# The gate's nonlinearity beside attention: a Silu lookup in place of tanh and a multiply

## The chip, the core and the metric

The kernel runs on one core of a Trainium2 chip. A core has five engines with queues of their own: TensorE (PE, matmuls; its weight loads are listed as PEld), VectorE (DVE), ScalarE (ACT), GpSimd (POOL) and SyncE (SP, which issues transfers). [...] Matmuls write to PSUM, a memory of banks[...]; the rest of the work is in SBUF. The metric is the device time of one execution in microseconds. A row of the profile names the line of the kernel and the tiles that it writes and reads (`hl<-sl,hh`).

## What is computed

The input has 4096 tokens of 256 features. The reference chains three residual blocks: half an FFN, attention, half an FFN again with the same weights.

```python
x = x + 0.5 * ffn(layernorm(x), ...)
x = x + attn(layernorm(x), ...)
x = x + 0.5 * ffn(layernorm(x), ...)

# in ffn
gate = jax.nn.silu(jnp.einsum('ech,ehi->eci', xg, rg))     # routed: 8 experts, top 2, capacity 640
up = jnp.einsum('ech,ehi->eci', xg, ru)
eout = jnp.einsum('eci,eih->ech', gate * up, rd)
...
shared = jax.nn.silu(x @ sg) * (x @ su) @ sd               # shared: 256 -> 2048 -> 256
return shared + SCALE * routed.reshape(b, s, h)

# in attn: groups of 64 tokens, 16 heads of 16
att = jnp.einsum('bghqd,bghkd->bghqk', q, k) * scale
att = jnp.where(causal, att, -jnp.finfo(att.dtype).max)
att = jax.nn.softmax(att, axis=-1)
y = jnp.einsum('bghqk,bghkd->bghqd', att, v)
```

silu(g) is g * sigmoid(g), which is also g/2 * (1 + tanh(g/2)).

## The kernel before

Tokens are worked on in blocks of 512 (`BT`) and tiles of 128. Every operand of a matmul is held as two fp16 planes, high and low, and a product is three matmuls (`TERMS`: high by high, high by low, low by high).

The program has four stages. Stage a: layernorm and routing of the first FFN (tiles `tile1`) with the shared FFN of blocks 0 to 3 beside them. Stage b: the eight experts of the first FFN. Stage c: attention (32 tiles, `tile2`, which also do layernorm and routing of the second FFN), with eleven blocks of shared FFN beside it: blocks 4 to 7 of the first FFN and 0 to 6 of the second. Stage d: the experts of the second FFN and the shared FFN of its last block. The change concerns stage c alone.

A block of the shared FFN is 16 chunks of 128 hidden features (`shared`). For a chunk, `gate_up` issues six matmuls for the gate into one PSUM tile `pgu`, then the nonlinearity into `sl`, then six matmuls for the up half into another `pgu`; line 319 multiplies the two on VectorE, line 321 casts to fp16 (`hh`, ScalarE), line 322 makes the low plane (`hl`, VectorE). The twelve down matmuls of a chunk (`down`, line 330) are issued one chunk late (`defer`), so that they follow the next chunk's gate and up. There are three PSUM tiles for `pgu`, two of `sl` and two pairs of `hh` and `hl`. A gate's PSUM tile is free for other matmuls when the last reader of the gate is done.

`gate_up` has two forms of the nonlinearity. With `tanh=True`, the form of stage c, ScalarE looks up tanh(g/2) (line 313), and VectorE computes (tanh + 1) * g from it (line 314); the factor 1/2 is folded into line 319. Otherwise ScalarE looks up Silu itself (line 317).

`attn_tile` is a generator: each `yield` ends a step of one attention tile. Its softmax subtracts the row maximum on GpSimd (line 550), takes the exponential on ScalarE (line 558, 128x1024), casts it to fp16 (line 560, ScalarE), makes the low plane on GpSimd (line 561) and transposes both by DMA (line 564). Other work of a tile on ScalarE: squares with a sum (line 498), casts of q and k (521, 527), copies of v (554, four of 64x512), layernorm's scaling (154) and casts (164, 505). `Tiles` starts a new tile every four slots, and `drive` takes two side steps for each step of the shared FFN and begins a slot every three.

Within the source order so given, the order on each engine is laid out by a scheduler when the kernel is built (`schedule_with_timeline_sim=True`, line 825); it also puts single matmuls of attention between those of a chunk.

ScalarE looks functions up in tables. The compiler puts an instruction that loads a table (ACT_TABLE_LOAD) ahead of a lookup where the loaded table lacks its function; the source has no such line, and the profile gives it the line of that lookup.

Of the kernel before, what the change touches and what calls it, by code (L numbers as in the profile page):

```python
# [14 lines left out]
AF = mybir.ActivationFunctionType  # L15
ALU = mybir.AluOpType
# [10 lines left out]
XP = UP * WS  # L27
# [10 lines left out]
class Net:  # L38
# [254 lines left out]
            R["sc"] = True  # L293
            self.tc.add_to_no_dep_group(R["key"], i)

    def gate_up(self, wc, x, h, tanh=False):

        nc = self.nc
        n = x.shape[-1]
        ps = []  # L300
        for i in range(2):
            p = self.ps_gu.tile([P, n], F32, name="pgu", tag="gu")
            j = 0
            for k in range(2):
                for (w, a) in TERMS:
                    nc.tensor.matmul(  # L306
                        p, lhsT=wc[:, w, i, k, :], rhs=x[:, 2 * a + k, :], start=(j == 0), stop=(j == 5))
                    j += 1
            ps.append(p)
            if i == 0:  # L310
                s = self.hp.tile([P, BT], F32, name="sl", bufs=self.nsl)[:, :n]
                if tanh:
                    nc.scalar.activation(s, p, AF.Tanh, scale=0.5 / XP)  # L313
                    nc.vector.scalar_tensor_tensor(  # L314
                        out=s, in0=s, scalar=1.0, in1=p, op0=ALU.add, op1=ALU.mult)
                else:
                    nc.scalar.activation(s, p, AF.Silu, scale=1.0 / XP)  # L317
                yield
        nc.vector.scalar_tensor_tensor(  # L319
            out=s, in0=ps[1], scalar=1.0 / XP / (2.0 * XP if tanh else 1.0), in1=s, op0=ALU.mult, op1=ALU.mult)  # L320
        nc.scalar.copy(h[0], s)  # L321
        nc.vector.tensor_tensor(out=h[1], in0=s, in1=h[0], op=ALU.subtract)  # L322
        yield
# [22 lines left out]
            res.append(r)  # L346
        return res

    def shared(self, b, xb, src, dst, tanh=False, late=2):
        nc = self.nc  # L350
        outs = [self.ps_out.tile([P, BT], F32, name="po", tag="po") for _ in range(2)]
        for c in range(16):
            if c == late:
                res = self.res_load(src, b)
            h = [a[:, 0:BT] for a in self.hbuf()]
            yield from self.gate_up(self.sgu[:, c], xb, h, tanh)

            def fin(c=c, h=h):
                self.down(outs, 4, h, self.sdw[:, :, c], c, 16)
                if c < 15:  # L360
                    return
                for i in range(2):
                    nc.vector.scalar_tensor_tensor(
                        out=res[i], in0=outs[i].rearrange("p (t f) -> p t f", f=H), scalar=0.5 / WS,
                        in1=res[i], op0=ALU.mult, op1=ALU.add)
                    nc.sync.dma_start(
                        out=dst[b * BT + i * 2 * P:b * BT + (i + 1) * 2 * P].rearrange("(t p) f -> p t f", p=P),
                        in_=res[i])

            self.defer(fin)  # L370
            yield
# [299 lines left out]
def run_slots(tiles, until):  # L671
    while not until():
        for _ in tiles.steps():
            pass


def drive(main, tiles, rate):

    credit = 0.0
    side = iter(())  # L680
    for _ in main:
        credit += 1.0
        for _ in range(2):
            if next(side, "end") == "end":
                break
        if credit >= rate:
            for _ in side:
                pass
            credit -= rate
            if not tiles.done():  # L690
                side = tiles.steps()
    for _ in side:
        pass


@with_exitstack
def macaron(ctx, tc, x, w_qkv, ln_w, w_proj, router_w, rg, ru, rd, sg, su, sd, out):
    nc = tc.nc
    x = x.rearrange("b s h -> (b s) h")
    out = out.rearrange("b s h -> (b s) h")  # L700
    n = Net(ctx, tc)
    R1 = n.route_init(0)
    R2 = n.route_init(1)
    R2["acc"] = out
    x2 = n.dr.tile([T, H], F32, name="x2")
    fbs = {}
    used = set()

    def new_fb(h, b):
        def get(t):  # L710
            if t == 0:
                assert h == 1 or (1, b) in used
                fb = fbs[(h, b)] = n.front_new()
                fb["pe"] = h == 1 and b < PEB
            return fbs[(h, b)]
        return get

    def tail(R, h, b, t):
        if t == 3:
            yield from n.route(R, b, fbs[(h, b)])  # L720

    def tile1(j):
        b, t = divmod(j, 4)
        y = n.load_tile(x, b, t)
        yield
        yield
        yield from n.front_steps(y, t, new_fb(1, b))
        yield from tail(R1, 1, b, t)

    def tile2(j):  # L730
        b, t = divmod(j, 4)
        yield from n.attn_tile(R1, j, x2 if b < NC else out, new_fb(2, b))
        yield from tail(R2, 2, b, t)

    def ready(h, b):
        return lambda: (h, b) in fbs and fbs[(h, b)]["n"] == 4

    def all_shared(key, b, src, dst, **k):
        yield from n.shared(b, fbs[key]["xb"], src, dst, **k)
        used.add(key)  # L740

    def fill(R):

        for e in range(E):
            z = n.raw.tile([P, 5, XW], F32, name="zero")
            nc.gpsimd.memset(z, 0.0)
            nc.vector.tensor_scalar_add(z[:, :, H], n.tokid[:, 0:5], float(T + e * CAP))
            nc.sync.dma_start(out=R["xg"][e * CAP:(e + 1) * CAP].rearrange("(t p) f -> p t f", p=P), in_=z)
            yield

    with n.phase("a", BT, 2, 10):
        n.ident = n.at.tile([P, P], F32, name="ident")
        make_identity(nc, n.ident)
        n.load_router(router_w)
        tiles = Tiles(tile1, 32, GAP_A)
        run_slots(tiles, ready(1, 0))
        n.load_shared(sg, su, sd)
        for _ in fill(R1):
            pass
        for b in range(NA):  # L760
            run_slots(tiles, ready(1, b))
            if b == 2:
                tiles.extra.append(fill(R2))
                for i in range(NA, NB):
                    nc.sync.dma_start(out=R1["acc"][i * BT:(i + 1) * BT], in_=x[i * BT:(i + 1) * BT])
            drive(all_shared((1, b), b, x, R1["acc"]), tiles, RATE_A)
        run_slots(tiles, tiles.done)
        cur = {}
        for _ in n.expert_load(R1, 0, cur):
            pass  # L770
    with n.phase("b", CAP, 3):
        n.experts(R1, rg, ru, rd, cur)
    with n.phase("c", BT, 2, 6, SLC):
        n.attn_init(w_qkv, ln_w, w_proj)
        tiles = Tiles(tile2, 32, GAP_C)
        for b in range(NA, NB):
            drive(all_shared((1, b), b, R1["acc"], R1["acc"], tanh=True), tiles, RATE_C)
        for b in range(NC):
            run_slots(tiles, ready(2, b))
            drive(all_shared((2, b), b, x2, R2["acc"], tanh=True), tiles, RATE_C)  # L780
        run_slots(tiles, tiles.done)
        cur = {}
        for _ in n.expert_load(R2, 0, cur):
            pass
    with n.phase("d", CAP, 3):
        n.experts(R2, rg, ru, rd, cur)
        for b in range(NC, NB):
            for _ in all_shared((2, b), b, out, out, late=10):
                pass
# [6 lines left out]
RATE_C = 3.0  # L796
# [33 lines left out]
```

## Time and profile before

| | us |
|---|---|
| median of 3 runs | 1857.15 (1856.97 to 1858.42) |
| the profiled execution | 1854.02 |
| its span, first to last instruction | 1852.2 |
| TensorE matmul busy | 1785.9 (96%) |
| VectorE busy | 1259.6 (68%) |
| ScalarE busy | 940.6 (51%) |
| GpSimd busy | 726.0 (39%) |

A profile is of one execution. "Busy" is the time in which an engine ran an instruction; matmuls are pipelined and their ends are modelled, so a busy TensorE is not one at its peak. The granted TensorE clock was 0.998 of full speed. Rows of the costliest groups name line, engine, operation, tiles, shapes and count; then busy us in total and mean ns of one; then the engine's idle time just ahead of them and what ended most of it. The groups of the gate's path in stage c and beside it:

```profile
L306 PE MATMUL pgu<-xb,sgu 128*128 128x512 f16 x3072 | 740.2, 381 | 19.5 <-DVE sl L314 8.5
L321 ACT CAST hh<-sl 128x512 f16<-128x512 f32 (+2 forms) x512 | 272.8, 533 | 540.8 <-DVE sl L319 535.5
L319 DVE SCALAR_TENSOR_TENSOR sl<-pgu,sl 128x512 f32<-128x512 f32 (+2 forms) x512 | 300.6, 587 | 203.4 <-PE pgu L306 183.2
L322 DVE TENSOR_TENSOR hl<-sl,hh 128x512 f16<-128x512 f32 (+2 forms) x512 | 328.4, 642 | 146.4 <-ACT hh L321 145.4
L317 ACT ACTIVATE sl<-pgu 128x384 f32<-128x384 f32 (+1 forms) x336 | 158.8, 473 | 53.8 <-PE pgu L306 30.4
L313 ACT ACTIVATE sl<-pgu 128x512 f32<-128x512 f32 x176 | 103.9, 591 | 36.5 <-PE pgu L306 35.1
```

Lines 306, 319, 321 and 322 hold the work of all stages; lines 313 and 314 that of stage c alone (176 = 11 blocks of 16 chunks).

### The profile page before, as it was taken

Reading aid. Unit: us, or ns where it says so; the run is one execution under the profiler, and the core shown is the slowest. Engines: PE = TensorE matmul, PEld = TensorE weight load, DVE = VectorE, ACT = ScalarE, POOL = GpSimd, SP = SyncE. Lnnn points to the kernel's source line nnn. Section 1 sums busy time; section 2 is a strip of 40 time slices with the busy share of each in tenths; the row PEclk is TensorE's granted clock in tenths of the full one; section 3 lists DMA queues with packets and bytes.
Section 4 is the critical chain, followed back from the end, with each engine's and each line's share of the span. In section 5 each row is a group of like instructions: output and inputs, shape, how many; then the busy total and the mean of one; then the engine's idle time right before and its main releaser. Section 6 shows DMA issues by size and latency. Waiting matters only on the chain.

```text
span 1852.2 us, 37412 instructions
## 1 busy us (share of the span) xinstructions
PE 1785.9 (96%) x13546; PEld 1189.7 (64%) x13546; DVE 1259.6 (68%) x3190; ACT 940.6 (51%) x1991; POOL 726.0 (39%) x943
## 2 busy tenths in 40 slices
PE   6899999999999899999999999999999999999999
PEld 3456557777777556665555656565665677777765
DVE  8666545566666567888888888788765566666643
ACT  4333334555555466666566666666433455555542
POOL 5664430123111334557667575757520011112210
PEclk9999999999999999999999999999999999999999
DMA  9763032555543345657576666756213044445420
GB/s 272 220 161 93 12 78 61 114 121 116 119 107 86 82 81 101 135 104 146 103 140 122 130 130 115 147 104 122 53 34 83 27 106 111 110 109 125 106 47 12
DMA packets 447513, 196.59 MB, mean 106 GB/s; under 512 B 302369, under 2 KB 444381, under 8 KB 447264
## 3 DMA queue, kind: packets, MB, share of 16 engines
q1 hardware_dynamic: 429664, 173.03, 41.6%
q0 software_dynamic: 17664, 21.17, 6.7%
q8 instruction: 106, 1.74, 0.4%
q14 instruction: 79, 0.65, 0.1%
HBM read 81.04 MB, written 52.85 MB: 72 GB/s over the span
## 4 chain that ended last, share of the span: by engine, by line
PE 59%; DVE 11%; POOL 9%; DMA 8%; issue 6%; ACT 4%; SPq 1%; DVEq 0%; POOLq 0%; ACTq 0%
PE pgu L306 38%; PE po L330 19%; POOL xg L287 3%; DVE hl L322 2%; DVE sl L319 2%; DMA xg<-X,di 2%; DVE sl L314 2%; DMA xg<-zero 1%; DMA y<-in_L_attn_x_dram 1%; DMA rs<-in_L_ffn_su_dram 1%; POOL X L285 1%; ACT hh L321 1%; DMA QT<-QK 1%; DVE st L139 1%; ACT V L554 1%
## 5 line engine op out<-in xcount | busy, mean ns | idle before, releaser
L306 PE MATMUL pgu<-xb,sgu 128*128 128x512 f16 x3072 | 740.2, 381 | 19.5 <-DVE sl L314 8.5
L321 ACT CAST hh<-sl 128x512 f16<-128x512 f32 (+2 forms) x512 | 272.8, 533 | 540.8 <-DVE sl L319 535.5
L306 PE MATMUL pgu<-xe,wc 128*128 128x384 f16 (+1 forms) x3072 | 497.1, 299 | 0.6
L306 PEld LDWEIGHTS <-sgu 128*128 128x128 f16 x3072 | 294.1, 98 | 298.1 <-issue 33.0
L319 DVE SCALAR_TENSOR_TENSOR sl<-pgu,sl 128x512 f32<-128x512 f32 (+2 forms) x512 | 300.6, 587 | 203.4 <-PE pgu L306 183.2
L322 DVE TENSOR_TENSOR hl<-sl,hh 128x512 f16<-128x512 f32 (+2 forms) x512 | 328.4, 642 | 146.4 <-ACT hh L321 145.4
L330 PEld LDWEIGHTS <-hh 128*128 128x128 f16 x3328 | 319.6, 98 | 114.8 <-ACT hh L321 18.4
L330 PE MATMUL po<-sdw,hh 128*128 128x256 f16 x2048 | 350.6, 273 | 10.8 <-ACT hh L321 10.0
L306 PEld LDWEIGHTS <-wc 128*128 128x128 f16 x3072 | 300.1, 98 | 94.6 <-issue 2.2
L330 PE MATMUL po<-sdw,hl 128*128 128x256 f16 x1024 | 250.9, 274 | 11.4 <-DVE hl L322 10.6
L330 PE MATMUL po<-wd,hh 128*128 128x256 f16 x1280 | 223.7, 273 | 0.0
L330 PEld LDWEIGHTS <-hl 128*128 128x128 f16 x1664 | 162.6, 98 | 62.3 <-DVE hl L322 28.5
L426 POOL DMA_INDIRECT out_dram<-eo,eid x40 | 64.6, 1616 | 315.2 <-DVE hl L322 247.1
L317 ACT ACTIVATE sl<-pgu 128x384 f32<-128x384 f32 (+1 forms) x336 | 158.8, 473 | 53.8 <-PE pgu L306 30.4
L287 POOL DMA_INDIRECT xg<-X,di x128 | 137.3, 1072 | 89.4 <-DVE di L266 29.9
L426 POOL DMA_INDIRECT acc<-eo,eid x40 | 64.6, 1615 | 261.9 <-DVE hl L322 222.3
L330 PE MATMUL po<-wd,hl 128*128 128x256 f16 x640 | 152.5, 273 | 1.1 <-DVE hl L322 1.1
L314 DVE SCALAR_TENSOR_TENSOR sl<-sl,pgu 128x512 f32<-128x512 f32 x176 | 120.1, 682 | 38.9 <-ACT sl L313 38.2
L100 ACT ACTIVATE wc<-re 128x512 f16<-128x512 f32 x128 | 80.5, 629 | 84.9 <-PE pgu L306 57.4
L313 ACT ACTIVATE sl<-pgu 128x512 f32<-128x512 f32 x176 | 103.9, 591 | 36.5 <-PE pgu L306 35.1
L101 DVE SCALAR_TENSOR_TENSOR wc<-re,wc 128x512 f16<-128x512 f32 x128 | 88.3, 690 | 28.2 <-ACT wc L100 28.0
L550 POOL TENSOR_TENSOR S<-S,amx 128x1024 f32<-128x1024 f32 x32 | 63.7, 1990 | 81.0 <-DVE amx L549 74.1
(140 smaller groups left out, 1718.8 us busy)
## 6 DMA issues: line engine op xcount, KB each, us to landing
re<-in_L_ffn_rg_dram SPq DMA_DIRECT2D x128, 128.0 KB
re<-in_L_ffn_ru_dram SPq DMA_DIRECT2D x128, 128.0 KB
re<-in_L_ffn_rd_dram SPq DMA_DIRECT2D x128, 128.0 KB
xg<-zero SPq DMA_DIRECT2D x16, 650.0 KB
y<-acc SPq DMA_DIRECT2D x64, 128.0 KB
y<-in_L_attn_x_dram SPq DMA_DIRECT2D x32, 128.0 KB
acc<-xr SPq DMA_DIRECT2D x16, 256.0 KB
out_dram<-xr SPq DMA_DIRECT2D x16, 256.0 KB
```

What stands on the lines that cost most here:

```text
L100: nc.scalar.mul(hi, src, WS)
L101: nc.vector.scalar_tensor_tensor(out=lo, in0=src, scalar=WS, in1=hi, op0=ALU.mult, op1=ALU.subtract)
L287: i = nc.gpsimd.indirect_dma_start(out=R["xg"][:, :], out_offset=bass.IndirectOffsetOnAxis(ap=di[:, t, k:k + 1], axis=0), in_=X, in_offset ...
L306: nc.tensor.matmul(p, lhsT=wc[:, w, i, k, :], rhs=x[:, 2 * a + k, :], start=(j == 0), stop=(j == 5))
L313: nc.scalar.activation(s, p, AF.Tanh, scale=0.5 / XP)
L314: nc.vector.scalar_tensor_tensor(out=s, in0=s, scalar=1.0, in1=p, op0=ALU.add, op1=ALU.mult)
L317: nc.scalar.activation(s, p, AF.Silu, scale=1.0 / XP)
L319: nc.vector.scalar_tensor_tensor(out=s, in0=ps[1], scalar=1.0 / XP / (2.0 * XP if tanh else 1.0), in1=s, op0=ALU.mult, op1=ALU.mult)
L321: nc.scalar.copy(h[0], s)
L322: nc.vector.tensor_tensor(out=h[1], in0=s, in1=h[0], op=ALU.subtract)
L330: nc.tensor.matmul(o, lhsT=h[a][:, t * P:(t + 1) * P], rhs=wd[:, w], start=(c == 0 and j == 0 and t % 2 == 0), stop=(c == nch - 1 and j == 2),
L426: i = nc.gpsimd.indirect_dma_start(out=R["acc"][:, :], out_offset=bass.IndirectOffsetOnAxis(ap=ids[:, t:t + 1], axis=0), in_=eo, in_offset ...
```

## The change

All calls of `gate_up` use the Silu lookup. The tanh lookup, its VectorE instruction and the parameter that chose them are gone, and the scalar of line 319 has no factor 1/2 to fold in.

```diff
-    def gate_up(self, wc, x, h, tanh=False):
+    def gate_up(self, wc, x, h):
...
             if i == 0:
                 s = self.hp.tile([P, BT], F32, name="sl", bufs=self.nsl)[:, :n]
-                if tanh:
-                    nc.scalar.activation(s, p, AF.Tanh, scale=0.5 / XP)
-                    nc.vector.scalar_tensor_tensor(
-                        out=s, in0=s, scalar=1.0, in1=p, op0=ALU.add, op1=ALU.mult)
-                else:
-                    nc.scalar.activation(s, p, AF.Silu, scale=1.0 / XP)
+                nc.scalar.activation(s, p, AF.Silu, scale=1.0 / XP)
                 yield
         nc.vector.scalar_tensor_tensor(
-            out=s, in0=ps[1], scalar=1.0 / XP / (2.0 * XP if tanh else 1.0), in1=s, op0=ALU.mult, op1=ALU.mult)
+            out=s, in0=ps[1], scalar=1.0 / XP, in1=s, op0=ALU.mult, op1=ALU.mult)
...
-    def shared(self, b, xb, src, dst, tanh=False, late=2):
+    def shared(self, b, xb, src, dst, late=2):
...
-            yield from self.gate_up(self.sgu[:, c], xb, h, tanh)
+            yield from self.gate_up(self.sgu[:, c], xb, h)
...
-            drive(all_shared((1, b), b, R1["acc"], R1["acc"], tanh=True), tiles, RATE_C)
+            drive(all_shared((1, b), b, R1["acc"], R1["acc"]), tiles, RATE_C)
...
-            drive(all_shared((2, b), b, x2, R2["acc"], tanh=True), tiles, RATE_C)
+            drive(all_shared((2, b), b, x2, R2["acc"]), tiles, RATE_C)
```

The exponential of attention (line 558) stays as it is, between the chunks of the shared FFN.

## The prediction

> **What bounds the kernel now.** I first read part 4 of the page (the chain that ended last): TensorE has 59% of the span there, the gate and up matmuls of line 306 alone 38%. Then the row of busy engines by stage, for the stage that the change touches. The shared FFN beside attention runs from 611 to 1464 us; attention tiles fill 675 to 1313 us of it. The three rows are that stage's start, its steady middle and its end without attention (busy us and instructions of TensorE, weight loads, VectorE, ScalarE, GpSimd; then clock, DMA share, GB/s):
>
> ```profile
> 611.00:700.00 89.00, 81.15 (x536) 46.70 (x535) 58.30 (x110) 48.45 (x101) 36.99 (x39) 1.00 0.46 94
> 700.00:1300.00 600.00, 577.56 (x4825) 359.72 (x4824) 498.75 (x1277) 376.75 (x773) 382.04 (x471) 1.00 0.64 122
> 1300.00:1464.00 164.00, 161.95 (x1088) 98.52 (x1084) 105.77 (x232) 56.19 (x98) 36.90 (x66) 1.00 0.20 47
> ```
>
> In the middle TensorE is busy 577.56 of 600 us (96%), VectorE 83%, ScalarE 63%. So at most 600 - 577.56 = 22.4 us can be won there by anything that leaves the matmuls alone, and 2 us in the end stretch; the 8 us of the start are the fill of the attention pipeline. Next the view of waits, for TensorE in the middle stretch (us in total, times, longest):
>
> ```profile
> PE po L330 <- DVE hl L322: 8.9, 18, 0.7
> PE pgu L306 <- DVE sl L314: 6.9, 13, 0.9
> PE py L572 <- DVE S L544: 3.3, 6, 0.5
> PE py L572 <- DVE qk L511: 2.1, 6, 0.7
> PE psc L541 <- DVE S L544: 1.0, 5, 0.2
> ```
>
> All five end on VectorE, none on ScalarE. That speaks for the change: it takes work off VectorE and puts it on ScalarE.
>
> **What goes.** Line 314, the second half of the tanh form:
>
> ```profile
> L314 DVE SCALAR_TENSOR_TENSOR sl<-sl,pgu x176: 637/682/691, 612.5 to 1464.4; 128x512 f32<-128x512 f32 x176
> ```
>
> 176 x 0.682 = 120.1 us of VectorE, 79.8 of them between 700 and 1300, where VectorE falls from 83% to (498.75 - 79.8) / 600 = 70%. The tanh lookup (line 313, 591 ns by the page) becomes a Silu lookup (line 317, the same 128x512 shape, 594 ns by the groups kept apart by shape): nothing. The scalar of line 319 changes at no cost. The gate's PSUM bank is now free after the lookup, where it had to wait for line 314 too. The 8.5 us that TensorE waited for line 314 over the whole stage (6.9 in the middle) go; what is late next at that place is the Silu itself, or the bank of the up half.
>
> **What is added.** Table loads. Line 558 is the softmax exponential, line 317 the Silu of the other stages:
>
> ```profile
> L558 ACT ACTIVATE S<-S x32: 1051/1057/1060, 677.4 to 1313.1; 128x1024 f32<-128x1024 f32 x32
> L558 ACT ACT_TABLE_LOAD  x1: 1283/1283/1283, 675.7 to 675.7; - x1
> ...
> L317 ACT ACT_TABLE_LOAD  x2: 1283/1283/1283, 22.5 to 1468.1; - x2
> ```
>
> From this: Silu's table was loaded at 22.5 us, tanh ran from 611.9 us without a load, so that table has tanh too. The first exponential needed another table (675.7), tanh went on in it, and Silu needed its own again at 1468.1. Squares, copies and Identity ran before and after 675.7 with no load, so they need none. Silu and the exponential are therefore in different tables. The exponentials lie some 21 us apart with several lookups of line 317 between them, so each of the 32 costs a load for itself and one for the Silu after it: 64, plus the first, is 65, against 3 now. 62 x 1.283 = 79.5 us more on ScalarE. Between 700 and 1300 it is 29 x 2 x 1.283 = 74.4 us: (376.75 + 74.4) / 600 = 75%.
>
> **Row against rule.** The Trainium skill speaks against this change. "ScalarE: Activation LUTs", section "Table sets: the hidden batching unit", tells to batch lookups by table set, and its section "What ACT_TABLE_LOAD costs" counts 1283 ns for the load plus some 1380 ns of drain, 2.66 us for every switch. By that, 62 x 2.66 = 165 us, and ScalarE in the middle is at (376.75 + 58 x 2.66) / 600 = 89%, the next limit after TensorE. The rows here show the load's 1283 ns and no drain: in the timeline of ScalarE the load at 675.74 starts 0.03 us after the instruction before it ends (675.50 + 0.21), and the one at 22.53 starts 0.02 us after the cast before it (22.12 + 0.39). I take 1.283; the page's figure is part of the high end.
>
> **What of the loads reaches TensorE.** A load is hidden if ScalarE idles at that point or if the result is not needed yet. At 675.74 the load ran while GpSimd still worked on S (to 677.32), so it need not wait for its activation's data. The load at 1468.07 came after 0.80 us of waiting for VectorE; so some do wait. The order around the exponential repeats every four tiles (some 84 us); I walked one such group by the timelines of ScalarE, VectorE and TensorE, with the order unchanged. This is its second tile (start, duration, idle before and its releaser):
>
> ```profile
> 1003.93 0.41 ACT L164 CAST yp<-Y 128x256 f16<-128x256 f32 x1 [0.49 <-DVE Y L578]
> 1005.94 1.06 ACT L558 ACTIVATE S<-S 128x1024 f32<-128x1024 f32 x1 [1.60 <-POOL S L550]
> 1006.90 0.58 ACT L313 ACTIVATE sl<-pgu 128x512 f32<-128x512 f32 x1
> 1007.38 1.04 ACT L560 CAST e<-S 128x1024 f16<-128x1024 f32 x1
> ...
> 1007.51 0.69 DVE L314 SCALAR_TENSOR_TENSOR sl<-sl,pgu 128x512 f32<-128x512 f32 x1 [0.66 <-ACT sl L313]
> ...
> 1008.26 1.46 PE L306 MATMUL pgu<-xb,sgu 128*128 128x512 f16 x6 [0.26 <-DVE sl L314]
> ```
>
> The first load fits into the 1.60 us of idle before the exponential. The second starts at about 1007.0, and Silu ends near 1008.9. TensorE gets its bank at 1008.2 now (end of line 314); then it is 1008.9: 0.65 us lost. In the first tile of the group (exponential at 982.19) both loads sit back to back with work, Silu ends at 986.7 instead of 984.0, but line 319 waits until 987.11 for the up matmuls: nothing is lost. In the third (1026.47) Silu ends near 1031.0 where line 314 ended at 1029.0, and TensorE wants the bank at 1030.43: 0.55 us. The chain behind it, cast hh and line 322, moves by about 2 us and has 2.6 and 2.0 us of slack before the down matmuls at 1033.13 and 1034.01. In the fourth (1045.12) hh ends at 1048.0 and is needed at 1049.70: nothing. So 1.2 us per four tiles, some 10 us for 32, is the low end of the loss.
>
> Queued behind the two loads are the fp16 cast of S (line 560, for which GpSimd and the transpose of the exponentials wait), the cast hh and the reads of the next gate. High end: every tile loses both loads less the one line 314 in its path, 2 x 1.283 - 0.682 = 1.88 us, 31 x 1.88 = 58 us; with the page's price (2 x 2.66 - 0.68) 31 x 4.64 = 144 us. I stay near the low end, since the walk is over rows of this very place, but take twice its value, 2.4 us per four tiles or 19 us. Reason: TensorE's stream mixes single attention matmuls between the chunks in a planned order (at 1007.40 to 1008.26 one gate matmul, one of line 603, six gate matmuls); this order is laid out anew for the changed durations, so the idle stretches need not stay where the walk used them.
>
> Against it stand gains: the 8.5 us of waits for line 314, less the 2 us (0.26 x 8) that the walk already counted, 6.5 us; and of the 10.1 us that TensorE waits for line 322 over the stage about half, 5 us, as VectorE's queue is shorter. Sum: 19 - 6.5 - 5 = +7 us. The profiled execution took 1854.02 us (span 1852.2 and 1.8 around it), the median of the three runs is 1857.15, 3.1 us more; the difference is put on the median: **1864 us**, slower by 0.4%. About 0.2% (3.7 us) is what this kernel's measurement can tell from no change.
>
> **Rivals.**
> - *VectorE's relief wins.* The loads stay in ScalarE's idle time (223 us of the middle 600), and of the 8.5 + 10.1 us of waits for lines 314 and 322 two thirds go, 12 us: 1857 - 12 = 1845 us. For it: every wait of TensorE above ends on VectorE, and half of the walked tiles lose nothing. Against it: the waits for lines 544 and 511 come from attention's own chain, and that chain gets longer by the loads.
> - *The loads come through.* Two loads, exponential and cast (1.28 + 1.06 + 1.04 + 1.28) make a block of 4.7 us, in which no hh and no gate is served; three PSUM banks for gate and up let TensorE run only a chunk and a half ahead (12 such matmuls run in 2.59 us in the chain). From the point where the block falls just ahead of a hh that the next down matmuls need, in at least two of three tiles: 31 x 1.88 x 2/3 = 39 us, less 0 to 5: 1893 us. For it: of the 29 exponentials of the middle only 6 had ScalarE waiting before them (9.7 us). Against it: the walk.
> - *No change*: 19 and 11.5 are small and uncertain; they can cancel: 1857 us.
> - *No loads at all*, because one table serves both: the load at 1468.1 excludes it.
>
> **Chances.** Forecast 0.44, loads come through 0.19, VectorE's relief 0.23, no change 0.14. The range from 1844 to 1890 leaves out a tenth at each side; the likeliest case alone has 1856 to 1874. Faster by over 0.2%: 0.26; within: 0.17; slower: 0.57.
>
> **What will show it.** Lines 313 and 314 gone; 256 Silu of 128x512 under line 317; 65 table loads; VectorE's total 1259.6 - 120.1 = 1139.5 us, ScalarE's 940.6 + 79.5 = 1020 us. In the waits of TensorE, line 306 should name ScalarE's sl (lookup of line 317) in place of line 314, with 10 to 25 us; line 330 waiting for ScalarE's hh would be the second rival. If TensorE between 700 and 1300 is above 97%, the relief has won. I am wrong in the mechanism if a load is followed by more than 0.1 us of idle that no wait explains, or if there are far fewer than 65.

## The result, and the profile after

The changed kernel takes **1918.08 us** (median of four runs, 1916.47 to 1924.45); the kernel before took 1857.79 beside it (four runs, 1856.97 to 1858.90). The ratio is 1.0331, with an interval from 1.0306 to 1.0355: slower by 61 us. The direction was forecast, the size was not; the time lies above the range. The profiled execution is the slowest of the four, 1924.45 us (span 1922.7), so its numbers are read for where time lies rather than for the last microseconds.

First the page of the changed kernel: busy time of the engines, then three of the costliest groups. The tanh form is gone, so the lines below it have moved up by five: the Silu lookup is line 312, the multiply of gate and up 314, the cast hh 316, hl 317, the down matmuls 325, the exponential 553, its fp16 cast 555 and its low plane on GpSimd 556.

```profile
PE 1797.5 (93%) x13546; PEld 1190.5 (62%) x13546; DVE 1174.5 (61%) x3014; ACT 1020.5 (53%) x2053; POOL 719.3 (37%) x943
...
L306 PE MATMUL pgu<-xb,sgu 128*128 128x512 f16 x3072 | 743.7, 381 | 47.9 <-ACT sl L312 31.7
...
L317 DVE TENSOR_TENSOR hl<-sl,hh 128x512 f16<-128x512 f32 (+2 forms) x512 | 363.2, 710 | 181.8 <-ACT hh L316 177.1
...
L556 POOL TENSOR_TENSOR e<-S,e 128x1024 f16<-128x1024 f32 x32 | 68.1, 2128 | 96.1 <-ACT e L555 96.1
```

ScalarE has 1020.5 us, as summed. VectorE has 1174.5, 35 more than summed: all of it is line 317 (363.2 against 328.4 us for the same 512 instructions). TensorE does the same work in a longer time; the gate's matmuls now idle 47.9 us ahead of them instead of 19.5.

The loads, from the two lines that they are booked to (duration, first and last start):

```profile
L553 ACT ACT_TABLE_LOAD  x32: 1283/1283/1283, 684.6 to 1382.2; - x32
...
L312 ACT ACT_TABLE_LOAD  x33: 1283/1283/1283, 23.0 to 1385.8; - x33
```

They are 65, each of 1283 ns. The last exponential now comes some 70 us later (its load at 1382.2; before, the exponential itself at 1313.1). Spread over the intervals between the 32 exponentials, a tile takes 22.50 us instead of 20.51. The steady stretch by the row of busy engines (columns as in the prediction):

```profile
700.00:1300.00 600.00, 538.52 (x4425) 330.20 (x4423) 409.72 (x1063) 414.90 (x764) 337.94 (x416) 1.00 0.59 113
```

TensorE is at 90% where it was at 96%, and no other engine has come near a limit: VectorE 68%, ScalarE 69%, GpSimd 56%. Nothing is saturated, and still everything is slower. What TensorE waited for in that stretch:

```profile
PE po L325 <- DVE hl L317: 22.9, 40, 2.3
PE pgu L306 <- ACT sl L312: 21.8, 25, 2.2
PE psc L536 <- DVE qk L506: 5.7, 9, 1.5
PE pgu L306 <- DVE sl L314: 4.8, 4, 1.2
```

The wait named as a sign, line 306 for ScalarE's sl, is there with 21.8 us. But this view shows only the last link of each wait. It does not tell why sl was late.

### The profile page after: what moved, and what is told of

Same layout as the page of the kernel before. It is cut to its first block, busy times and chain, and to the rows that moved or that the text cites. A ratio compares the mean times of both kernels' runs of the same rounds, so it can differ in the third digit from the quotient of the medians.

```text
span 1922.7 us, 37358 instructions
## 1 busy us (share of the span) xinstructions
PE 1797.5 (93%) x13546; PEld 1190.5 (62%) x13546; DVE 1174.5 (61%) x3014; ACT 1020.5 (53%) x2053; POOL 719.3 (37%) x943
## 4 chain that ended last, share of the span: by engine, by line
PE 54%; DVE 12%; issue 11%; ACT 10%; DMA 6%; POOL 5%; SPq 1%; POOLq 0%; DVEq 0%; ACTq 0%
PE pgu L306 35%; PE po L325 17%; DVE hl L317 2%; DVE sl L314 2%; ACT L312 2%; ACT L553 2%; ACT V L549 1%; DMA rs<-in_L_ffn_su_dram 1%; ACT sl L312 1%; DVE amx L544 1%; POOL xg L287 1%; DVE st L139 1%; DMA y<-in_L_attn_x_dram 1%; ACT hh L316 1%; ACT S L553 1%
## 5 line engine op out<-in xcount | busy, mean ns | idle before, releaser
L306 PE MATMUL pgu<-xb,sgu 128*128 128x512 f16 x3072 | 743.7, 381 | 47.9 <-ACT sl L312 31.7
L317 DVE TENSOR_TENSOR hl<-sl,hh 128x512 f16<-128x512 f32 (+2 forms) x512 | 363.2, 710 | 181.8 <-ACT hh L316 177.1
L312 ACT ACTIVATE sl<-pgu 128x512 f32<-128x512 f32 (+2 forms) x512 | 263.9, 516 | 84.8 <-PE pgu L306 54.4
L556 POOL TENSOR_TENSOR e<-S,e 128x1024 f16<-128x1024 f32 x32 | 68.1, 2128 | 96.1 <-ACT e L555 96.1
L549 ACT COPY V<-vs 64x512 f16<-64x512 f16 x128 | 78.9, 616 | 18.0 <-PE py L567 15.1
```

Source lines behind the costliest of these rows:

```text
L306: nc.tensor.matmul(p, lhsT=wc[:, w, i, k, :], rhs=x[:, 2 * a + k, :], start=(j == 0), stop=(j == 5))
L549: nc.scalar.copy(V2[d * 64:(d + 1) * 64, g, :, :, 0:32], vs[g * 64:(g + 1) * 64].rearrange("p l (j c) -> p l j c", c=32))
L556: self.anchor = nc.gpsimd.tensor_tensor(out=e16[:, :, 1, :], in0=S, in1=e16[:, :, 0, :], op=ALU.subtract)
```

## The experiments

All ratios are to the kernel before, run on the same chip in the same job; 1% is 18.6 us.

**1. Loads and order taken apart.** The change does three things at once: it adds loads, it takes a VectorE instruction away, and it has the order laid out anew. In three kernels the order of the kernel before was kept, and only then the instructions were exchanged; a fourth takes the loads out of the new order. Where a lookup is made tanh without the second half of its form, the gate is tanh alone: such a kernel is built for its time and computes another function.

```diff
# x1: after the order is laid out, the 176 tanh lookups
+ ins[k] = copy.replace(i, func=AF.Silu)
# x1b: x1, and the second half of the tanh form on 8 elements, in place
+ o = copy.replace(o, ap=(o.ap[0], (1, 8)), ...)
+ ins[k] = copy.replace(i, outs=(o,), ins=(o, i.ins[1], o), op0=ALU.mult, op1=ALU.max)
# x1c: the short instruction alone, lookups stay tanh: no loads
# x2: the changed kernel, its order kept, lookups of stage c made tanh: no loads
+ ins[k] = copy.replace(i, func=AF.Tanh)
```

> The kernel before, with the order of all instructions laid out as it was; only then are the 176 tanh lookups of stage c turned into Silu lookups, so that 62 table loads of 1.283 us come in between instructions whose order is unchanged. Line 314 stays as it is, so the gate's value is another one. Theory A (the loads' own time on ScalarE is what costs, whatever the order): 1910 to 1930 us. Theory B (the walk over the old order was right, and the order laid out anew around the loads is what costs): 1862 to 1880 us.

> As the run before, but line 314 is reduced in place to 8 elements that keep their value, and the scalars are Silu's: the change as it was walked through in the prediction, in the old order, with the right result. Theory A: 1900 to 1920 us. Theory B: 1855 to 1870 us, the prediction's 1864 before any price for a new order was 1857.

> The old order, tanh lookups kept (so no loads), line 314 reduced in place to 8 elements; the gate is tanh alone. What VectorE's relief is worth by itself in the old order: both theories expect 1843 to 1853 us, and 1857 if the relief is worth nothing.

> The changed kernel with its own new order; only after it is laid out are the 176 Silu lookups of stage c turned into tanh lookups, so that 62 table loads drop out and nothing else moves; the gate is tanh alone. Theory A: 1840 to 1860 us. Theory B: 1890 to 1912 us, since the order stays.

| order | without loads | with loads | the 62 loads cost |
|---|---|---|---|
| before's | x1c: 0.9923 [0.9906, 0.9939] | x1b: 1.0173 [1.0156, 1.0190] | 2.50% = 46 us |
| after's | x2: 0.9892 [0.9875, 0.9908] | after: 1.0331 [1.0306, 1.0355] | 4.39% = 81 us |

x1, loads with line 314 at its full length, is 1.0231 [1.0214, 1.0248]. (x1 with 1905.38 us and x1b with 1892.59 lie 5 and 7 us under the ranges of theory A and 25 and 23 above those of B; x1c and x2 lie in A's.) So the relief of VectorE is real (14 us in the old order; x2, 20 us, has the new order besides), and the new order is by itself no fault: without loads it is the best of the four. The whole loss is the loads. In the old order they cost 46 us, in the new one 81, which is as much as their whole duration (62 x 1.283 = 79.5). Per tile the same: the exponentials of x2 are 20.02 us apart, those of the changed kernel 22.50, and two loads are 2.57 us. In the new order nearly every microsecond of a load lengthens a tile by a microsecond.

That needs a chain of steps, each waiting for the one before, that is as long as the tile's period. One view of the profile follows such a chain: from the last instruction back, at each step to what released it. Its shares in the stretch, first x2, then the changed kernel:

```profile
by line: PE pgu L308 29.1%; PE po L329 14.8%; issue 7.6%; DVE hl L321 5.8%; DVE sl L318 3.8%; PE pqk L602 3.7%; DVE S L543 2.4%; PE py L571 2.3%; DVE Y L577 2.1%; PE pao L602 2.0%; PE pv L602 1.9%; POOL ss L500 1.5%; DVE M L245 1.4%; POOL X
```

```profile
by line: issue 15.3%; PE pgu L306 9.9%; DVE hl L317 5.4%; ACT L312 5.3%; DVE sl L314 5.0%; PE po L325 4.5%; ACT L553 4.4%; ACT V L549 3.4%; DVE amx L544 3.2%; ACT sl L312 3.0%; POOL xg L287 2.7%; DVE S L539 2.2%; DVE st L139 2.2%; POOL ss L
```

Without loads TensorE's gate, up and down matmuls are 44% of the chain. With them they are 14%, and the loads themselves stand in it (5.3% and 4.4%). One tile of the changed kernel, cut from the same view (start, length, engine, tile and line):

```profile
1044.28 0.99 ACT L553
...
1045.57 0.02 ACT S L553
...
1046.94 1.28 ACT L312
...
1048.24 0.60 ACT sl L312
1048.83 0.94 ACT e L555
...
1049.85 2.13 POOL e L556
1051.98 0.95 POOL X L285 x4
...
1055.52 1.29 POOL xg L287
...
1057.45 0.74 POOL ss L496
...
1058.62 0.48 DVE qk L506
...
1062.80 1.13 DVE amx L544
...
1065.91 0.04 ACT yp L164
```

The next load for an exponential starts at 1066.34, and between 1044.28 and there no piece belongs to TensorE. ScalarE's cast of the exponentials (line 555) releases GpSimd's low plane (556). Behind that, in GpSimd's queue, stand a routing step (285), two gathers (287) and the scale ss of another tile's q and k (496), for which VectorE waits; its queue leads back to ScalarE, and there to the next load.

This is not the only way round. The tile after it:

```profile
1066.34 1.28 ACT L553
...
1068.70 1.28 ACT L312
...
1070.00 0.61 ACT sl L312
...
1070.63 0.07 DVE sl L314
...
1072.44 1.85 DVE hl L317
...
1076.26 2.59 PE pgu L306 x12
```

Here the link behind Silu's load is not the cast but Silu's value, for which the multiply of line 314 waits at its place in VectorE's queue, and 9.3 us of the tile are TensorE's. Of the 28 tiles from 747 us to the last but one, all have Silu's load in the chain; the cast is the next link in 6, Silu's value for VectorE in 22. From 836 to 1345 us one tile in four has TensorE in its chain and three have none. So both loads stand in a loop of ScalarE, VectorE and GpSimd that leads from tile to tile, mostly without TensorE, and by more than one way.

The ScalarE part of the first tile, by its timeline:

```profile
1044.28 1.28 ACT L553 ACT_TABLE_LOAD   x1
1045.57 1.06 ACT L553 ACTIVATE S<-S 128x1024 f32<-128x1024 f32 x1
1046.54 0.39 ACT L164 CAST yp<-Y 128x256 f16<-128x256 f32 x1
1046.94 1.28 ACT L312 ACT_TABLE_LOAD   x1
1048.24 0.60 ACT L312 ACTIVATE sl<-pgu 128x512 f32<-128x512 f32 x1
1048.73 1.04 ACT L555 CAST e<-S 128x1024 f16<-128x1024 f32 x1
```

Both loads lie ahead of the cast. GpSimd's waits for this cast: before, 17.0 us in 23 waits; x2 and the changed kernel:

```profile
POOL e L560 <- ACT e L559: 29.1, 23, 2.6
```

```profile
POOL e L556 <- ACT e L555: 79.4, 26, 4.5
```

**2. Is it the gate's bank?** The rival theory: the gate's path alone, where a later Silu holds its PSUM bank. A fourth bank for gate and up, taken from attention, would help then.

```diff
- self.ps_gu = pool("ps_gu", 3, space=PSUM)
+ self.ps_gu = pool("ps_gu", 4, space=PSUM)
- self.ps_m = pool("pm", 5 - nout, space=PSUM)
+ self.ps_m = pool("pm", 4 - nout, space=PSUM)
```

> The changed kernel with four PSUM banks for gate and up and two for attention. If the gate's bank that waits for the late Silu is what carries the loads to TensorE (27 us of its waits name it): 60 us of difference to the control shrink to 25 to 40 us. If ScalarE's queue carries them by other ways (late casts, late attention steps): still 50 to 70 us over the control.

> The kernel before with four PSUM banks for gate and up in place of three, and two in place of three for attention's matmuls; laid out anew. A control for the next run: 1850 to 1870 us; more if attention needs its third bank.

1.0332 [1.0315, 1.0350] for the changed kernel, 1.0005 [0.9996, 1.0013] for the one before. Nothing is won: the wait of line 306 for sl falls to 14.0 us, and waits of attention's matmuls for line 506 and others take its place. By itself this does not clear the bank, since the bank was taken from attention, the other suspect: a tile takes 23.27 us in place of 22.50 (in the control 22.36 in place of 20.51), and that may hide a gain. Run 5 says more.

**3. Number and place of the loads, in the order of before.** d makes the lookups Silu only in every second interval between exponentials, p only the last lookup of each interval, so that Silu's load moves away from the cast, to just ahead of the next exponential's load.

```diff
# d, p: in x1b, which lookups become Silu, by interval k between exponentials
+ name for k, r in enumerate(runs) for name in (r if k % 2 else ())        # d
+ name for k, r in enumerate(runs) for name in r[-1:]                      # p, inner intervals
```

> The old order with line 314 reduced, as in x1b, but Silu lookups only after every second exponential and tanh lookups after the others: 30 loads more than in x1c in place of 62 (the gates of the other half are tanh alone). x1c took 1846 us, x1b 1893. If every load costs the same (theory A): half, 1868 to 1872 us. If the cost comes from a ring in which one late tile delays the next (theory C), single tiles recover in the tile between: under 1860 us.

> The old order with line 314 reduced, but of the lookups between two exponentials only the last one is a Silu (the others tanh alone), so that there are as many loads as in x1b, but the load for Silu is gone from the place between the exponential and the cast of its result and stands before the next exponential. If it is the pair of loads around the exponential that holds up the gate there and the fp16 cast that GpSimd waits for (theory C): 1865 to 1880 us. If only the sum of ScalarE's time counts (theory A): 1888 to 1896 us, as x1b.

d, with 32 of the 62 loads, is 1.0013 [1.0005, 1.0022], 0.90% over x1c: fewer loads cost less than in proportion (half of 2.50% would be 1.25%), so a part of the price only comes when every tile has it. p is 1.0052 [1.0036, 1.0069], 1.29% over x1c. With as many loads as x1b it loses half as much, and GpSimd's wait for the cast falls from 56.7 us to 18.8. (1864.53 us is half a microsecond under the range of theory C, 23 under that of A.) Place matters as much as number.

**4. Place alone, in the new order.** The changed kernel with its order kept; only lookups between an exponential and its cast become tanh, so that Silu's load comes behind the cast. The 62 added loads stay.

```diff
+ elif between and i.name in LOOKUPS:      # between: after Exp, before its cast
+     ins[k] = copy.replace(i, func=AF.Tanh)
```

> The changed kernel in its own order, as it was laid out; only then are the lookups between an exponential and the fp16 cast of its result turned into tanh (one of some five per tile; their gate is tanh alone). The count of loads stays, but the load for Silu moves from ahead of the cast to behind it. Theory A (each load's time counts wherever it stands): 1912 to 1920 us. Theory C (a load costs where it delays a chain of attention steps through ScalarE and GpSimd that is as long as a tile's period): 32 x 1.28 = 41 us less, some 1875 to 1885 us.

1.0089 [1.0072, 1.0105] against 1.0331: 2.42%, **45 us, come back by moving a load past one lookup and one cast** (1870.30 us, 5 under the range of theory C). In the changed kernel a load stood between exponential and cast in 29 of the 32 tiles, here in none; from the start of an exponential to that of its cast the mean falls from 2.85 us to 1.57, and 32 x 1.28 is 41 us. A tile takes 21.10 us. The timeline of ScalarE in this kernel:

```profile
1017.38 1.06 ACT L557 ACTIVATE S<-S 128x1024 f32<-128x1024 f32 x1
...
1018.64 0.59 ACT L314 ACTIVATE sl<-pgu 128x512 f32<-128x512 f32 x1
1019.13 1.03 ACT L559 CAST e<-S 128x1024 f16<-128x1024 f32 x1
...
1020.70 1.28 ACT L314 ACT_TABLE_LOAD   x1
```

Over x2 it is still slower by 1.97% = 37 us. The other 32 loads stand directly ahead of the exponentials, in the same chain; 31 of them are 39.8 us. That this remainder is theirs fits, but no run moved them. This run moves the load past the first lookup as well as past the cast, and so does p; which of the two carried the loss no run tells apart. The chain of the changed kernel names both. GpSimd's wait for the cast is no measure of it: it is 48.8 us here, and 24.0 in g4 of after, which loses as much as the changed kernel with its 79.4.

**5. The chain's other links shortened, loads kept.** If attention's chain sets the period, it must help to shorten it anywhere. The low plane of the exponentials (m), and the subtraction of the row maximum too (m2), move from GpSimd to VectorE; the order is laid out anew.

```diff
-        self.anchor = nc.gpsimd.tensor_tensor(out=e16[:, :, 1, :], in0=S, in1=e16[:, :, 0, :], op=ALU.subtract)
+        nc.vector.tensor_tensor(out=e16[:, :, 1, :], in0=S, in1=e16[:, :, 0, :], op=ALU.subtract)
# m2: also
-        self.anchor = nc.gpsimd.tensor_tensor(
+        nc.vector.tensor_tensor(
             out=S, in0=S, in1=mx...
```

> The changed kernel with the low plane of the exponentials (line 556, 2.13 us a tile) made on VectorE in place of GpSimd. The loads stay as they are. Theory C (a chain of a tile's steps through ScalarE, GpSimd's queue and VectorE sets the pace, and the loads are links of it): a link of it gets shorter by 0.9 us and leaves GpSimd's queue, 20 to 45 us less than the changed kernel, 1873 to 1898 us. Theory A: unchanged, 1910 to 1925 us, or more, since VectorE gets 39 us of work.

> As the run before, and the subtraction of the row maximum (line 545, 1.90 us) on VectorE too. Theory C: 40 to 70 us less than the changed kernel, 1848 to 1878 us; under 1853 it would beat both kernels. Theory A: 1910 to 1930 us.

> The kernel before with the low plane of the exponentials on VectorE. A control: VectorE, at 83% beside attention, gets 39 us more, GpSimd 68 us less: 1850 to 1880 us. If this alone is faster than the kernel before by as much as m_after than the changed kernel, the chain is not a matter of the loads.

> The kernel before (tanh form, three loads) with both attention steps, the subtraction of the row maximum and the low plane, on VectorE. If the chain of attention steps is still near TensorE's pace after the first of them moved: 2 to 10 us under that run's 0.990 of the kernel before. If VectorE, then at some 90% beside attention, is the next limit: at or above 0.990, 1840 to 1860 us.

| | before | after |
|---|---|---|
| as it is | 1 | 1.0331 [1.0306, 1.0355] |
| m | 0.9903 [0.9886, 0.9919] | 1.0078 [1.0061, 1.0095] |
| m2 | 0.9859 [0.9842, 0.9875] | 1.0004 [0.9995, 1.0013] |

The changed kernel wins 47 and 61 us, with all its loads in it; TensorE's waits for sl fall from 21.8 to 3.6 and 5.1 us, those for hl from 22.9 to 7.9 and 1.3, with the same three banks for gate and up. So the wait for the bank was a symptom for the most part. The loads did not move away from the cast to bring this about: from an exponential's start to its cast's the mean is 2.54 and 2.99 us, 2.85 in the changed kernel. The kernel before wins 18 and 26 us; for m, meant as a control, 1850 to 1880 us had been expected, and it took 1840.35: its chain was near the limit too. Against their own controls the loads and the relief of VectorE together still cost 1.8% (m) and 1.5% (m2), in place of 3.3%. These runs also end the disturbance of VectorE by GpSimd (below), so a part of the win could be that. But x2 and s have the long line 317 too (means of 1132 and 1152 ns, 1148 in the changed kernel) and are faster than the changed kernel by 81 and 45 us. The groups by shape in the stretch, before and then m2 of before:

```profile
L322 DVE TENSOR_TENSOR hl<-sl,hh 128x512 f16<-128x512 f32 x116 | 104.0, 896 | 19.0 <-ACT hh L321 18.5
```

```profile
L322 DVE TENSOR_TENSOR hl<-sl,hh 128x512 f16<-128x512 f32 x122 | 89.2, 731 | 5.0 <-ACT hh L321 4.6
...
L550 DVE TENSOR_TENSOR S<-S,amx 128x1024 f32<-128x1024 f32 x30 | 40.7, 1358 | 0.0
...
L561 DVE TENSOR_TENSOR e<-S,e 128x1024 f16<-128x1024 f32 x30 | 37.3, 1245 | 0.9 <-ACT e L560 0.9
```

**m2 of before, 1829.23 us, is the fastest kernel of this study.** It keeps the tanh form, and TensorE is busy for 595 of the 600 us, VectorE for 540.

**6. A longer period.** `RATE_C` sets how many steps of the FFN come to a slot of attention. At 3.5 a tile has more TensorE work beside it, under which a longer chain could hide.

```diff
-RATE_C = 3.0
+RATE_C = 3.5      # r375: 3.75
```

> The changed kernel with RATE_C 3.5. Theory A (a load holds TensorE up for its own time): 55 to 65 us over the control, 1905 to 1920 us. Theory C (the chain of a tile, 23.06 us with the loads, is longer than TensorE's 20.6 us of work per tile): TensorE has 23.2 us of work per tile now and covers the chain: 1845 to 1875 us.

> The kernel before with RATE_C 3.5 in place of 3.0: 4.67 chunks beside each attention tile in place of 4, so that attention reaches into the stretch of stage c that it left free. A control for the next two: TensorE's work per tile is some 2.6 us more, so every other queue has that much more time for it: 1843 to 1860 us.

> The changed kernel with RATE_C 3.75: 5 chunks per tile, 24.5 us of TensorE's work. Theory A: as above, 1905 to 1920 us. Theory C: covered with 1.4 us to spare, 1842 to 1862 us, unless the last attention tiles come too late for the block that needs them (then longer, with TensorE idle at the end of stage c).

r35 is 1.0268 [1.0251, 1.0285] after and 1.0093 [1.0076, 1.0110] before, so the change costs 1.75% over its own control in place of 3.31%. r375 is 1.0369 [1.0352, 1.0387], without a control. In absolute times all three missed what was expected (1871.03, 1903.93 and 1921.66 us; the ranges, for the changed kernel those of theory C, end at 1860, 1875 and 1862), and the last two come within 2 us of the range of theory A; but the difference to the control, 33 us, is far from its 55 to 65. The stretched attention reaches the end of stage c, and there something else is lost, in the control too; the longest of TensorE's waits in r35 of before, from 611 to 1490 us:

```profile
PE pgu L306 <- ACT wc L100: 21.7, 2, 21.0
```

One wait of 21.0 us for the experts' weights, which ends at 1483 us; from 1400 to 1480 the granted clock is 0.87. r35 and r375 of after have the same wait with 20.5 and 21.1 us, so it accounts for much of the miss in absolute times, but not for the 1.75% that is left between r35 and its control. The half that came back fits the chain; but the order is another one too, with a load ahead of the cast in 16 tiles in place of 29, and the two were not taken apart.

**7. The end of the stage.** Silu only in the last block of stage c, which runs after attention and needs no extra loads.

```diff
- drive(all_shared((2, b), b, x2, R2["acc"]), tiles, RATE_C)
+ drive(all_shared((2, b), b, x2, R2["acc"], tanh=b < NC - 1), tiles, RATE_C)
```

> The kernel before, with the Silu lookup only in the last of the eleven blocks of stage c, which begins after the last exponential: three loads as before, 16 instructions of line 314 less. TensorE is the limit there: 0 to 3 us less than before, 1851 to 1857 us.

1.0001 [0.9992, 1.0010]: sixteen of line 314 gone, and nothing won that can be told from the noise. In this last block VectorE's relief is worth nothing.

## Why the prediction was wrong

**Right: what the change does.** 65 loads on the two lines at 1283 ns without a drain, and ScalarE's sum of 1020 us (measured 1020.5). In ScalarE's timeline above, Silu's load begins within 0.02 us of the end before it, and each lookup follows its load within 0.02 us.

**Right in the sum, by luck in one term: the gains.** The prediction had 6.5 us for the waits for line 314 and 5 us for half of those for line 322, 11.5 us. x1c, that edit alone in the old order, measured 14 us. Its waits in the stretch, where the prediction's list had 8.9, 6.9, 3.3, 2.1 and 1.0 us:

```profile
PE po L333 <- DVE hl L325: 8.3, 13, 0.8
PE pgu L307 <- DVE sl L316: 2.3, 7, 0.4
PE psc L544 <- DVE S L547: 1.1, 6, 0.2
```

The waits for line 314 (316 here) fall by two thirds. Those for line 322 (325 here) hardly fall; in their place 5.4 us of waits of line 572 for attention's own steps on VectorE went, which had no term.

**Off by 35 us: VectorE's sum.** Line 317 became longer, 710 ns in the mean where it had 642. x2 has this too, so it comes with the new order and not with the loads. x2 is the fastest of the four kernels of run 1 with it; what it costs was not measured.

**The step that failed: what of the loads reaches TensorE.** The walk over one group of four tiles gave 10 us, and 19 after doubling it for a new order. Measured are 46 us in the very order that was walked and 81 in the new one. The walk asked of each delayed instruction only whether the next matmul of the gate's path waited for it, inside one tile. It named the cast of the exponentials and GpSimd as standing behind the loads and gave them no price, and of a late Silu it did not ask what stands behind the multiply in VectorE's queue. The delay of the cast goes through GpSimd's queue, ss, VectorE and the next softmax to the next exponential, that of Silu's value through VectorE's queue. There it meets that tile's own two loads: in this chain, delays add up from tile to tile. Such a loss is not found in one tile, since in one tile nothing need wait; it shows in the period. The idle 1.60 us ahead of an exponential into which a load was fitted is slack of ScalarE, not of the chain. Doubling the walk for a new order was the right doubt and far too little.

The trace of the kernel before had the sign. The prediction read the chain on the page, which covers the whole program; there gate, up and down matmuls are 57% (lines 306 and 330). The same view for 700 to 1300 us:

```profile
by line: PE pgu L306 13.3%; issue 12.9%; POOL xg L287 7.7%; PE po L330 6.8%; DVE hl L322 4.5%; DVE sl L314 4.1%; DVE sl L319 3.5%; POOL X L285 2.9%; DMA QT<-QK 2.4%; POOL e L561 2.1%; POOL S L550 1.9%; POOL ss L501 1.8%; DVE S L544 1.8%; AC
```

They are 20% here, and in the four tiles that were walked, 982 to 1066 us, the chain has no piece of TensorE at all, though TensorE is 96% busy in the stretch. There attention's loop was already as long as the period and had no room for two more loads per tile.

**The high end and the rival.** "The loads come through" charged 1.88 us in two of three tiles and gave 1893, near x1b (1892.59) by coincidence. Its carrier, the gate's bank and the cast hh ahead of the down matmuls, was in the main not the cause (run 5; run 2 alone does not tell). Its 1.88 us were too few as well: the period grew by 2.48 us from x2 to the changed kernel. The relief of VectorE and the new order took back some 20 of 81 us.

**What stays open.** The exponentials' own loads were not moved, and the cast and Silu's value were not delayed one without the other. Nor is it settled why the same loads cost 35 us more in the new order than in the old: a load stands ahead of the cast in 28 of 32 tiles there and in 29 here, so it is not their place at the cast, and the rest of the two orders was not compared tile by tile.

## What to carry to other kernels

Before pricing an insertion on an engine with spare time, follow what it delays once around the loop, through every in-order queue, until it comes back to itself, and compare that length with the period; busy shares and the busiest engine's waits do not show such a loop; the chain of waits, taken for the stretch concerned and not for the whole program, does. On a loop that is near the period an added microsecond can cost a microsecond (81 us for loads of 79.5 in the new order), whatever idle time lies beside it, and the place ahead of a result for which another in-order queue waits was the dearest one here. It also pays to shorten such a loop where another engine does the same step faster, as the two softmax steps did here.

## What was not expected of the hardware

- GpSimd takes 2133 ns for the low plane of 128x1024 exponentials and 1990 for the subtraction; VectorE took 1245 and 1358 ns for the same.
- VectorE's 128x512 low plane (hl) has a mean of 896 ns in the kernel before and up to 1152 in the new order, where GpSimd does both softmax steps, and 686 to 753 ns in the four kernels that move one or both of these steps to VectorE. What in GpSimd's work causes it was not measured by itself.
- Sixty-two table loads of 1283 ns each cost 24 us at the end where Silu's stands next to the exponential's (p), 46 where it stands ahead of the cast (x1b), and 81 in the changed kernel's order, where it stands ahead of the cast too.
